# Smaller key tiles, larger table tiles and earlier splits at the start of a TensorE-bound attention

## The chip, the core and the metric

The kernel runs on one core of one Trainium2 chip. The metric is the device time in microseconds of one execution, as the median of several runs. A profile of one execution gives every instruction of the five engines (PE is TensorE, DVE is VectorE, ACT is ScalarE, POOL is GpSimd, SP is SyncE, which here only issues transfers) and every DMA. PEld is the loading of TensorE's weights, which overlaps its matmuls. The names ACT and DVE are used below as the profile uses them.

## What is computed

Eight images of 32 x 32 tokens with 384 channels pass through two layers. The start of the first layer is what matters here:

```
x = x + conv_attn(group_norm(x))
    qkv  = x @ qkv_w + qkv_b                 # 6 heads of 64
    attn = (q / 8) @ k.T                     # 1024 x 1024 per head
    attn += rel_h[query, key row] + rel_w[query, key column]
            # rel_h = q . rel_pos_h[hq - hk + 31], rel_w likewise
    x    = softmax(attn) @ v @ proj_w + proj_b
t = t + causal_attention(layer_norm(t))      # one head of 384
t = t + ffn(layer_norm(t))                   # sign weights; only images 0 to 4
```

## The kernel before, in words

An image b goes through layer 0 (projections, position tables, attention with 6 heads in 3 pairs), layer 1's attention, and for b = 0 to 4 through the FFN. Everything is fp32 or a pair of rounded values: q and k are each cut into a high part and the remainder, so that scores are the sum of three products: k with q, ks (k with its two parts exchanged) with q, and a fixed matrix `unit` with r, the position terms.

**PSUM.** Two pools: `ps_s` has 2 tiles of two banks (s tiles, 128 x 1024 in fp32), `ps_o` has 4 tiles of one bank (o tiles, 128 x 512).

**Projections of q and k** (`queries_keys`, L443). For m = 0 to 2 (q, one pair of heads each) and 3 to 5 (k), `project_T` (L383, matmuls L388) fills an s tile with 6 matmul instructions (12 records in the profile, since a matmul in full fp32 appears as two). Then for each half of 512 tokens ACT writes the high part with the bias (L453, two instructions of 64x512, one a head), and DVE writes the remainder from the same bank (L456, two instructions), which reads ACT's result. For k the parts are then copied by SP's transfers to `ks`.

**Position tables** (`positions`, L470). For a pair and a head (par) two o tiles of 512 queries are computed (L479) from q and a fixed table. ACT copies the upper 64 rows (L483) and DVE the lower 64 in column order (L484) into a page, which a transfer puts into DRAM (L488, `far`). Four transfers then read the diagonals back into one page `near` (L495), whose rows of 128 bytes put each query's 32 + 32 relevant values in place.

**Splits** (`split`, L500). `near` of a pair is cut into a high part, ACT's cast (L506), and a remainder, DVE's subtract (L507), both of 32x1024, four of each a pair, written into r. Those with d = 1 exchange rows and columns while they read. Pairs 0 and 1 are split next to the values; pair 2 is `later`, which the attention calls after its first group of products with v, except in image 0.

**Values** (`values`, L511). Eight blocks of 128 tokens in o tiles (L398), copied by ACT and DVE in turn (L512).

**Attention** (`attend0_fast`, L545). For each of 8 chunks of keys and each head of the pair: scores in an s tile (L554), exp on ACT into a page (L558), sums on DVE (L567), and two chunks behind, the products with v (L572).

**Order.** The source order gives each instruction its priority, and a scheduler fixes one stream for each engine. On its engine an instruction waits for those ahead of it. So an ACT instruction whose input is late holds up every ACT instruction behind it. The first q projections of image b + 1 are put into the stream of TensorE while image b's FFN ends. Its closing step (`finish`, L919 on DVE after L915 on POOL, then the output transfer L948) runs in the middle of the next image's projections, as `unfinished`. A function of another table set costs ACT an ACT_TABLE_LOAD: GELU (L854) and exp (L558) do, one after the other, in images 0 to 4 and the image that follows.

`multiply_out` (L282) computes wq @ wk.T once, in image 0, for layer 1: two loads and 9 matmul instructions; before, it comes at the end of image 0's projections.

Of the kernel before, what the change touches and what calls it, by code (L numbers as in the profile page):

```python
# [17 lines left out]
P = 128  # L18
# [56 lines left out]
def conv_attn_hybrid(  # L75
# [203 lines left out]
        nc.vector.tensor_tensor(pb, pb, ps[:, :C], ALU.add)  # L279


    def multiply_out(pools):  # L282
        both = pools.flat("wqkT")
        wqT_sb, wkT_sb = (both[:, i * NC * C : (i + 1) * NC * C].rearrange("p (k c) -> p k c", k=NC) for i in range(2))
        nc.sync.dma_start(out=wqT_sb, in_=wqT.rearrange("(k p) c -> p k c", p=P))
        nc.sync.dma_start(out=wkT_sb, in_=wkT.rearrange("(k p) c -> p k c", p=P))
        for m in range(NC):
            ps = pools.o_tile(f"wqk_{m}")
            for k in range(NC):
                nc.tensor.matmul(ps[:, :C], wqT_sb[:, k, ts(m, P)], wkT_sb[:, k, :], start=(k == 0), stop=(k == NC - 1))  # L290
            nc.vector.tensor_scalar_mul(wqk[:, m, :], ps[:, :C], C**-0.5)

    def stages(pools):
# [140 lines left out]
        def layer0(b, xT):  # L434

            q, k, ks, r = ([pools.image(f"{n}_{b}_{par}", F32R) for par in range(2)] for n in ("q", "k", "ks", "r"))

            rows = (slice(0, HD), slice(HD, P))

            def queries_keys(m):  # L443
                p = m % NPAIR
                bias = bqk[:, m : m + 1]
                ps = project_T(wqkv_sb, ts(m, P), xT, f"qk_{b}_{m}")
                dst = [(q if m < NPAIR else k)[par][:, p, :] for par in range(2)]

                for half in range(2):
                    t = ts(half, T // 2)  # L450
                    for par in range(2):
                        hi = rows[par]
                        nc.scalar.activation(dst[par][hi, t], ps[hi, t], AF.Identity, bias=bias[hi])  # L453
                    for par in range(2):
                        hi, lo = rows[par], rows[1 - par]
                        nc.vector.scalar_tensor_tensor(  # L456
                            dst[par][lo, t], ps[hi, t], bias[hi], dst[par][hi, t].bitcast(F32), ALU.add, ALU.subtract
                        )
                if m >= NPAIR:
                    for par in range(2):  # L460
                        for i in range(2):
                            nc.sync.dma_start(
                                out=ks[par][rows[i], p, :].bitcast(F32), in_=dst[par][rows[1 - i]].bitcast(F32)
                            )

            def positions(p):  # L470

                fars = []
                for par in range(2):
                    page = pools.page(f"far_{b}_{p}_{par}")
                    by_col = page.rearrange("i (w h) -> i w h", h=H)
                    for half in range(2):
                        ps = pools.o_tile(f"rel_{b}_{p}_{par}_{half}")
                        for i in range(2):
                            nc.tensor.matmul(  # L479
                                ps, rel_split[:, i].rearrange("d a n -> d (a n)"), q[par][:, p, ts(half, 512)],  # L480
                                start=(i == 0), stop=(i == 1),
                            )
                        nc.scalar.copy(page[:HD, ts(half, 512)], ps[:HD])  # L483
                        nc.vector.tensor_copy(  # L484
                            by_col[HD:, :, ts(half, H // 2)], ps[HD:].rearrange("i (h w) -> i w h", w=W)
                        )
                    far = store.tile([P, T], F32, tag=f"far_{p}_{par}", bufs=2, name=f"{pools.path}_far_{b}_{p}_{par}")
                    nc.sync.dma_start(out=far, in_=page)  # L488
                    fars.append(far)
                near = pools.page(f"near_{b}_{p}")  # L490
                for par in range(2):
                    start = fars[par][0:1, 0:1]
                    for d in range(2):
                        src = bass.AP(start.tensor, start.offset + d * HD * T, [[T, 32], [T + 32, 32], [1, 32]])
                        nc.sync.dma_start(  # L495
                            out=near[ts(2 * par + d, 32)].rearrange("m (n o) -> m n o", n=32), in_=src
                        )
                return near

            def split(p, near):  # L500
                for d in range(2):
                    for par in range(2):
                        hi, lo = 2 * par + d, 2 * (1 - par) + d
                        dst = r[par][:, p, :].rearrange("k (h w) -> k h w", h=H)
                        src = near[ts(hi, 32)].rearrange("k (w h) -> k h w" if d else "k (h w) -> k h w", h=H)
                        nc.scalar.copy(dst[ts(hi, 32)], src)  # L506
                        nc.vector.tensor_tensor(dst[ts(lo, 32)], src, dst[ts(hi, 32)].bitcast(F32), ALU.subtract)  # L507

            v = pools.flat(f"v0_{b}")[:, : NJ * C].rearrange("p (j c) -> p j c", j=NJ)

            def values(j):  # L511
                (nc.vector.tensor_copy if j % 2 else nc.scalar.copy)(  # L512
                    v[:, j, :], project(wqkv_sb, slice(2 * C, 3 * C), xT, j, f"v0_{b}_{j}")
                )

            near = []
            for m in range(2 * NPAIR):
                queries_keys(m)
                if 0 < m <= NPAIR:
                    near.append(positions(m - 1))  # L520
                if m == NPAIR and unfinished:
                    unfinished.pop()()
            split(0, near[0])
            for j in range(NJ):
                values(j)
            split(1, near[1])

            later = [lambda: split(2, near[2])]
            if b == 0 or not pools.fast:
                later.pop()()  # L530
            if pools.fast and b == 0:
                join_biases(pools)
                multiply_out(pools)

            def residual():
                xt = load_x(pools, b)
                nc.gpsimd.tensor_tensor(xt, xt, pb.unsqueeze(1).to_broadcast([P, NJ, C]), ALU.add)
                return xt
# [4 lines left out]
            return (attend0_fast if pools.fast else attend0_general)(residual, b, sides, v, later)  # L543

        def attend0_fast(residual, b, sides, v, later):  # L545


            oT = pools.image(f"oT_{b}")
# [75 lines left out]
            for p in range(NPAIR):  # L624
                sums = [pools.page(f"sum0_{b}_{p}_{par}") for par in range(2)]
                avs = None
                pending = []
                for c in range(NJ):
                    prs = [scores(p, c, par) for par in range(2)]
                    if c == 0:  # L630
                        first = prs
                    if c == 1:
                        if p > 0:
                            few = set_aside(p - 1, *last)
                        if p == 0 and b > 0:
                            xt = residual()
                        avs = [pools.o_tile(f"av0_{b}_{p}_{half}") for half in range(2)]
                    if b == 0 and (p, c) >= (0, 1) and xt is None and next(signs, True):
                        xt = residual()
                    if len(pending) == 2:  # L640
                        values(p, pending, sums, avs)
                        if later:
                            later.pop()()
                        if c == 4 and p > 0:
                            divide(p - 1, few)
                        pending = []
                    pending.append((c, prs))
                values(p, pending, sums, avs)
                last = (sums, avs)
# [18 lines left out]

            return xt, more

        def attend0_general(residual, b, sides, v, later):
            state = {}
            xt = residual()

# [173 lines left out]
        def ffn(xt, b):  # L848
# [71 lines left out]

            return add

        unfinished = []

        def run(pools):
            gn = load_T(0)
            if pools.fast:
                load_weights(pools)
            gn = group_norm_T(0, gn)
            if pools.fast:  # L930
                make_unit()
# [70 lines left out]
```

## Time and profile before

Three runs took 2600.14, 2606.68 and 2608.02 us; the median is 2606.68. The profiled execution has a span of 2599.5 us and a mean granted TensorE clock of 0.996.

| from the profile | |
|---|---|
| matmuls of q and k (L388) | 576 records, 261.5 us |
| matmuls of layer 0's scores (L554) | 3 x 768 records, 746.9 us |
| products with v (L572) | 1536 records, 359.7 us |
| exp of layer 0 (L558, ACT) | 384 instructions, 393.0 us |
| splits: ACT (L506), DVE (L507) | 96 of each, 145.9 and 193.7 us |
| transfers of k to ks | 96 of 256 KB, 5.1 us to landing |
| near, read from far | 96 of 128 KB, 3.9 us to landing |
| first projection of images 0 to 7 starts at | 16.9, 305.3, 654.5, 1003.6, 1352.4, 1700.4, 2048.3, 2319.8 us |

How to read it: a group's line has the source line, the engine and the operation, the tile written and the tiles read, the shape, then the busy time in us, the mean of one instruction in ns, and the engine's idle time just before these instructions, with what ended it. In a list of waits a line says which instruction of which engine waited for which other; numbers are the total in us, how often, and the longest. Idle time matters only on the engine that sets the end. An image with an FFN before it takes about 348 us, one without 271 to 280 (from the starts in the table).

### The profile page before, as it was taken

The page shows a single profiled execution, that of the slowest core. Times are in us where ns is not written, and L with a number is a line of the kernel's source. Part 1 is how long each engine was busy: PE and PEld are TensorE (multiplying, and loading weights), DVE is VectorE, ACT ScalarE, POOL GpSimd, SP SyncE. Part 2 cuts the span into 40 slices and gives each one's busy share as a digit, 9 for nine tenths or more (in the row PEclk, how much of TensorE's full clock was granted, in tenths as well). Part 3 has the DMA queues.
Part 4 walks back from the last instruction along what each step waited for, and adds up shares of the span by engine and source line. Part 5 has one row for each costly group of instructions (what it writes and reads, how often), then busy time and mean ns, then how long its engine had stood idle before and what let it go on. Part 6 is the DMA issues. An engine that isn't in the chain of part 4 may idle for free. (4 is left out here: it accounts for less than half of the span.)

```text
span 2599.5 us, 25162 instructions
## 1 busy us (share of the span) xinstructions
PE 2521.0 (97%) x9538; PEld 1508.4 (58%) x9538; DVE 1619.4 (62%) x2407; ACT 1157.0 (45%) x1513; POOL 115.5 (4%) x106
## 2 busy tenths in 40 slices
PE   7999998999999999999999999999999999999998
PEld 4555685555765556755557555576555555555554
DVE  5895468763587644786545776347864486538652
ACT  4641377421666314764127643156641264127420
POOL 1000002000001000010000100000100010001000
PEclk9999999999999999999999999999999999999999
DMA  6431106011042101150110601003200240015000
GB/s 167 147 146 61 37 1 170 1 61 37 1 117 54 49 13 37 41 130 1 61 37 1 170 1 61 6 31 91 80 25 1 67 104 1 25 39 131 1 1 26
DMA packets 148993, 144.72 MB, mean 56 GB/s; under 512 B 107264, under 2 KB 129664, under 8 KB 147328
## 3 DMA queue, kind: packets, MB, share of 16 engines
q1 hardware_dynamic: 142928, 119.36, 16.4%
q0 software_dynamic: 2880, 23.59, 2.6%
q8 instruction: 77, 1.26, 0.2%
q10 hardware_dynamic: 3056, 0.08, 0.1%
q14 instruction: 52, 0.43, 0.1%
HBM read 75.38 MB, written 42.47 MB: 45 GB/s over the span
## 5 line engine op out<-in xcount | busy, mean ns | idle before, releaser
L558 ACT ACTIVATE f_pr<-f_s 128x1024 f32<-128x1024 f32 x384 | 393.0, 1027 | 403.2 <-PE f_s L554 370.3
L567 DVE TENSOR_TENSOR f_sum<-f_sum,f_pr 128x1024 f32<-128x1024 f32 x288 | 349.0, 1244 | 147.0 <-ACT f_pr L558 145.6
L572 PE MATMUL f_av<-f_pr,f_v 128*64 128x512 f32 x1536 | 359.7, 599 | 0.0
L554 PE MATMUL f_s<-f_q,f_k 128*128 128x512 f32 x768 | 258.5, 418 | 21.8 <-ACT f_pr L558 14.9
L388 PE MATMUL f_qk<-f_gnT,wqkv_sb 128*128 128x512 f32 x576 | 261.5, 598 | 8.2 <-DVE f_k L456 5.6
L554 PE MATMUL f_s<-f_q,f_ks 128*128 128x512 f32 x768 | 245.3, 401 | 0.0
L554 PE MATMUL f_s<-f_r,unit 128*128 128x512 f32 x768 | 243.1, 398 | 0.0
L572 PEld LDWEIGHTS f_av<-f_pr,f_v 128*64 128x64 f32 x1536 | 103.2, 136 | 202.8 <-issue 195.0
L507 DVE TENSOR_TENSOR f_r<-f_near,f_r 32x1024 fp32r<-32x1024 f32 x96 | 193.7, 2017 | 29.0 <-ACT f_r L506 26.3
L554 PEld LDWEIGHTS f_s<-f_q,f_k 128*128 128x128 f32 x768 | 125.8, 189 | 137.9 <-issue 50.3
L762 PE MATMUL f_s<-f_q,f_lnT 128*128 128x512 f32 (+3 forms) x576 | 201.4, 491 | 0.0
L776 PE MATMUL f_av<-f_v,f_pr 128*128 128x385 f32 x576 | 194.5, 486 | 0.0
L388 PEld LDWEIGHTS f_qk<-f_gnT,wqkv_sb 128*128 128x128 f32 x576 | 108.0, 191 | 124.3 <-issue 114.0
L554 PEld LDWEIGHTS f_s<-f_q,f_ks 128*128 128x128 f32 x768 | 145.6, 190 | 35.9
L554 PEld LDWEIGHTS f_s<-f_r,unit 128*128 128x128 f32 x768 | 145.8, 190 | 34.8
L776 PEld LDWEIGHTS f_av<-f_v,f_pr 128*128 128x128 f32 x576 | 108.6, 190 | 78.6 <-issue 11.5
L506 ACT CAST f_r<-f_near 32x1024 fp32r<-32x1024 f32 x96 | 145.9, 1520 | 2.3
L398 PE MATMUL f_v<-wqkv_sb,f_gnT 128*128 128x384 f32 x384 | 129.4, 490 | 10.5 <-ACT f_v L512 8.3
L762 PEld LDWEIGHTS f_s<-f_q,f_lnT 128*128 128x128 f32 x576 | 100.1, 190 | 67.7 <-issue 43.5
L877 DVE TENSOR_REDUCE am<-f_h 128x1 f32<-128x1024 f32 (+2 forms) x80 | 71.6, 946 | 96.6 <-ACT f_h L870 96.6
L770 ACT ACTIVATE f_pr<-f_s 128x1024 f32<-128x1024 f32 (+3 forms) x64 | 41.7, 651 | 202.0 <-DVE f_s L767 202.0
L870 ACT ACTIVATE f_h<-f_y,b_sb 128x256 f32<-128x256 f32 x240 | 100.8, 472 | 67.0 <-PE f_y L866 67.0
(163 smaller groups left out, 3360.6 us busy)
## 6 DMA issues: line engine op xcount, KB each, us to landing
f_far<-f_far SPq DMA_DIRECT2D x48, 512.0 KB, 2.9
f_ks<-f_k SPq DMA_DIRECT2D x96, 256.0 KB, 5.1
f_gnT<-in_xT SPq DMA_DIRECT2D x24, 512.0 KB, 4.5
f_near<-f_far SPq DMA_DIRECT2D x96, 128.0 KB, 3.9
f_x<-in_x SPq DMA_DIRECT2D x32, 384.0 KB, 6.4
out_y<-f_x SPq DMA_DIRECT2D x32, 384.0 KB, 3.8
f_w1a<-w1s POOLq DMA_DIRECT2D x5, 1536.0 KB, 7.2
f_w2a<-w2s POOLq DMA_DIRECT2D x5, 1536.0 KB, 6.6
```

The lines of the kernel that those rows point to most:

```text
L388: nc.tensor.matmul(ps[:, half, :], w[:, k, cols], xT[:, k, ts(half, 512)], start=(k == 0), stop=(k == NC - 1),)
L398: nc.tensor.matmul(ps[:, :C], xT[:, k, ts(j, P)], w[:, k, cols], start=(k == 0), stop=(k == NC - 1))
L506: nc.scalar.copy(dst[ts(hi, 32)], src)
L507: nc.vector.tensor_tensor(dst[ts(lo, 32)], src, dst[ts(hi, 32)].bitcast(F32), ALU.subtract)
L554: nc.tensor.matmul(sc[:, half, :], keys[:, ts(c, P)], queries[:, ts(half, 512)], start=(i == 0), stop=(i == 2))
L558: nc.scalar.activation(pr, sc.rearrange("p a n -> p (a n)"), AF.Exp)
L567: nc.vector.tensor_tensor(sums[par], prev, prs[par], ALU.add)
L572: nc.tensor.matmul(avs[half][ts(par, HD), :], v[:, c, ts(h, HD)], prs[par][:, ts(half, 512)], start=(c == 0), stop=(c == NJ - 1),)
L762: nc.tensor.matmul(sc[:, half, lo:], xT[:, c // 4, k, ts(c % 4, P)], q[:, half, k, lo:], start=(k == 0), stop=(k == NC - 1),)
L776: nc.tensor.matmul(av[:, : C + 1], prs[c][:, ts(j - c, P)], v[:, c, :], start=(c == 0), stop=(c == j))
L870: nc.scalar.activation(pairs[i][:, m, :, :], ps[:, ts(i % 2, 256)].rearrange("p (j q) -> p j q", j=2), AF.Identity, bias=b1_sb[:, m : m + 1],)
L877: nc.vector.tensor_reduce(am[:, i, n - 1 : n], pairs[i][:, cuts[n - 1] : cuts[n], :, :], AX.XYZ, ALU.max, apply_absolute_value=True)
```

## The change

It rearranges what lies between an image's first projection and its first exponentials, so that TensorE finds its tiles and operands ready.

1. k, and in image 0 also q, is projected by halves into one-bank o tiles, so that ACT can take one half while DVE is at another. q of the other images stays in s tiles.
2. The table products of pairs 1 and 2 (in image 0 of all pairs) go to two-bank s tiles, and one ACT copy of 64x1024 and one DVE copy take the place of two each.
3. The splits of pairs 1 and 2 work on 64 rows at a time for both heads (`split_both`): two ACT copies and two DVE subtracts a pair into the pages of far, which are free by then, and eight transfers of 32x1024 from there into r. `near` is laid out by d for this. All splits stand ahead of the attention; `later` is gone. Pair 0 keeps `split`, called after the fifth projection.
4. After the previous image's closing step a one-element exp brings exp's table in (images 1 to 5).
5. wq and wk are loaded at the very start, and `multiply_out` runs after image 0's fifth projection.

```diff
-    def multiply_out(pools):
+    def load_qk(pools):
...
+        return wqT_sb, wkT_sb
+
+    def multiply_out(pools, wqT_sb, wkT_sb):
...
             def queries_keys(m):
                 p = m % NPAIR
                 bias = bqk[:, m : m + 1]
-                ps = project_T(wqkv_sb, ts(m, P), xT, f"qk_{b}_{m}")
                 dst = [(q if m < NPAIR else k)[par][:, p, :] for par in range(2)]
 
+                both = project_T(wqkv_sb, ts(m, P), xT, f"qk_{b}_{m}") if b and m < NPAIR else None
                 for half in range(2):
                     t = ts(half, T // 2)
+                    if both is None:
+                        ps = pools.o_tile(f"qk_{b}_{m}_{half}")
+                        for i in range(NC):
+                            nc.tensor.matmul(
+                                ps, wqkv_sb[:, i, ts(m, P)], xT[:, i, t], start=(i == 0), stop=(i == NC - 1)
+                            )
+                    else:
+                        ps = both[:, t]
...
             def positions(p):
 
-                fars = []
+                fars, pages = [], []
                 for par in range(2):
                     page = pools.page(f"far_{b}_{p}_{par}")
+                    pages.append(page)
                     by_col = page.rearrange("i (w h) -> i w h", h=H)
-                    for half in range(2):
-                        ps = pools.o_tile(f"rel_{b}_{p}_{par}_{half}")
...
+
+                    n = 1 + (p > 0 or b == 0)
+                    for part in range(2 // n):
+                        ps = pools.s_tile(f"rel_{b}_{p}_{par}") if n == 2 else pools.o_tile(f"rel_{b}_{p}_{par}_{part}")[:, None, :]
...
+                        ps = ps.rearrange("p a n -> p (a n)")
+                        nc.scalar.copy(page[:HD, ts(part, n * 512)], ps[:HD])
                         nc.vector.tensor_copy(
-                            by_col[HD:, :, ts(half, H // 2)], ps[HD:].rearrange("i (h w) -> i w h", w=W)
+                            by_col[HD:, :, ts(part, n * H // 2)], ps[HD:].rearrange("i (h w) -> i w h", w=W)
                         )
...
+                        at = 2 * d + par if p else 2 * par + d
+                        nc.sync.dma_start(out=near[ts(at, 32)].rearrange("m (n o) -> m n o", n=32), in_=src)
+                return near, [page.bitcast(F32R) for page in pages]
+
+            def split_both(p, near, pages):
+
+                for d in range(2):
+                    hi, lo, src = (t[ts(d, HD)].rearrange("k (h w) -> k h w", h=H) for t in (*pages, near))
+                    if d:
+                        src = near[ts(d, HD)].rearrange("k (w h) -> k h w", h=H)
+                    nc.scalar.copy(hi, src)
+                    nc.vector.tensor_tensor(lo, src, hi.bitcast(F32), ALU.subtract)
+                for i in range(2):
+                    for d in range(2):
+                        for par in range(2):
+                            nc.sync.dma_start(
+                                out=r[par][ts(2 * i + d, 32), p, :].bitcast(F32),
+                                in_=pages[i][ts(2 * d + par, 32)].bitcast(F32),
+                            )
...
                 queries_keys(m)
                 if 0 < m <= NPAIR:
                     near.append(positions(m - 1))
+                if m == NPAIR + 1 and sides_qk:
+                    multiply_out(pools, *sides_qk.pop())
                 if m == NPAIR and unfinished:
                     unfinished.pop()()
-            split(0, near[0])
+
+                    early = pools.small.tile([P, 1], F32, tag="early", name=f"early0_{b}")
+                    nc.scalar.activation(early, k[1][:, 0, T - 1 :].bitcast(F32), AF.Exp, scale=0.0)
+                if m == NPAIR + 1:
+                    split(0, near[0][0])
             for j in range(NJ):
                 values(j)
-            split(1, near[1])
-
-            later = [lambda: split(2, near[2])]
-            if b == 0 or not pools.fast:
-                later.pop()()
+            split_both(1, *near[1])
+            split_both(2, *near[2])
             if pools.fast and b == 0:
                 join_biases(pools)
-                multiply_out(pools)
...
                     if len(pending) == 2:
                         values(p, pending, sums, avs)
-                        if later:
-                            later.pop()()
...
             if pools.fast:
                 load_weights(pools)
+                sides_qk.append(load_qk(pools))
```

More of the change, by code (lines that the diff above doesn't have):

```diff
@@ L445, in queries_keys @@
                 bias = bqk[:, m : m + 1]
-                ps = project_T(wqkv_sb, ts(m, P), xT, f"qk_{b}_{m}")
                 dst = [(q if m < NPAIR else k)[par][:, p, :] for par in range(2)]
+                both = project_T(wqkv_sb, ts(m, P), xT, f"qk_{b}_{m}") if b and m < NPAIR else None
                 for half in range(2):
                     t = ts(half, T // 2)
+                    if both is None:
[6 more added lines that the diff above has]
+                        ps = both[:, t]
                     for par in range(2):
                         hi = rows[par]
-                        nc.scalar.activation(dst[par][hi, t], ps[hi, t], AF.Identity, bias=bias[hi])
+                        nc.scalar.activation(dst[par][hi, t], ps[hi], AF.Identity, bias=bias[hi])
                     for par in range(2):
@@ L456, in queries_keys @@
                         nc.vector.scalar_tensor_tensor(
-                            dst[par][lo, t], ps[hi, t], bias[hi], dst[par][hi, t].bitcast(F32), ALU.add, ALU.subtract
+                            dst[par][lo, t], ps[hi], bias[hi], dst[par][hi, t].bitcast(F32), ALU.add, ALU.subtract
                         )
@@ L470, in positions @@
             def positions(p):
-                fars = []
+                fars, pages = [], []
                 for par in range(2):
                     page = pools.page(f"far_{b}_{p}_{par}")
+                    pages.append(page)
                     by_col = page.rearrange("i (w h) -> i w h", h=H)
-                    for half in range(2):
-                        ps = pools.o_tile(f"rel_{b}_{p}_{par}_{half}")
[L478 to L483, printed above, removed]
+                    n = 1 + (p > 0 or b == 0)
+                    for part in range(2 // n):
+                        ps = pools.s_tile(f"rel_{b}_{p}_{par}") if n == 2 else pools.o_tile(f"rel_{b}_{p}_{par}_{part}")[:, None, :]
+                        for half in range(n):
+                            for i in range(2):
+                                nc.tensor.matmul(
+                                    ps[:, half, :], rel_split[:, i].rearrange("d a n -> d (a n)"),
+                                    q[par][:, p, ts(part + half, 512)], start=(i == 0), stop=(i == 1),
+                                )
+                        ps = ps.rearrange("p a n -> p (a n)")
+                        nc.scalar.copy(page[:HD, ts(part, n * 512)], ps[:HD])
                         nc.vector.tensor_copy(
-                            by_col[HD:, :, ts(half, H // 2)], ps[HD:].rearrange("i (h w) -> i w h", w=W)
+                            by_col[HD:, :, ts(part, n * H // 2)], ps[HD:].rearrange("i (h w) -> i w h", w=W)
                         )
@@ L494, in positions @@
                         src = bass.AP(start.tensor, start.offset + d * HD * T, [[T, 32], [T + 32, 32], [1, 32]])
[L495 to L498, printed above, removed]
+                        at = 2 * d + par if p else 2 * par + d
[8 more added lines that the diff above has]
+                    nc.vector.tensor_tensor(lo, src, hi.bitcast(F32), ALU.subtract)
+                for i in range(2):
+                    for d in range(2):
[3 more added lines that the diff above has]
+                                in_=pages[i][ts(2 * d + par, 32)].bitcast(F32),
+                            )
             def split(p, near):
@@ L542, in layer0, with attend0_fast @@
                       for par in range(2)] for p in range(NPAIR)]
-            return (attend0_fast if pools.fast else attend0_general)(residual, b, sides, v, later)
-        def attend0_fast(residual, b, sides, v, later):
+            return (attend0_fast if pools.fast else attend0_general)(residual, b, sides, v)
+        def attend0_fast(residual, b, sides, v):
             oT = pools.image(f"oT_{b}")
@@ L669, in attend0_fast, with attend0_general @@
             return xt, more
-        def attend0_general(residual, b, sides, v, later):
+        def attend0_general(residual, b, sides, v):
             state = {}
@@ L921, in ffn @@
             return add
+        sides_qk = []
         unfinished = []
```

## The prediction

> **What bounds the kernel.** First the page's part 1, then the waits of PE (total us, times, longest), then the groups, then the timeline of one image's start.
>
> ```profile
> PE 2521.0 (97%) x9538; PEld 1508.4 (58%) x9538; DVE 1619.4 (62%) x2407; ACT 1157.0 (45%) x1513; POOL 115.5 (4%) x106
> ```
>
> ```profile
> PE f_s L554 <- ACT f_pr L558: 14.9, 13, 1.9
> ...
> PE f_v L398 <- ACT f_v L512: 8.3, 8, 1.1
> PE f_qk L388 <- DVE f_k L456: 5.6, 5, 2.3
> ...
> PE f_s L554 <- DVE f_k L456: 4.1, 5, 0.8
> ...
> PE f_s L554 <- ACT f_far L483: 2.8, 3, 0.9
> PE f_v L398 <- DVE f_far L484: 2.2, 5, 0.4
> ...
> PE f_qk L388 <- DVE f_q L456: 1.5, 5, 0.3
> ```
>
> TensorE does its 2521 us whatever happens; only its idle 78.5 us can be won. The seven waits shown, all between an image's projections and its first exponentials, sum to 39.4 us. The groups say why (busy, mean ns, then idle before):
>
> ```profile
> L453 ACT ACTIVATE f_k<-f_qk,bqk 64x512 fp32r<-64x512 f32 x96 | 65.5, 683 | 86.9 <-DVE f_k L456 56.0 <-PE f_qk L388 29.8
> L456 DVE SCALAR_TENSOR_TENSOR f_k<-f_qk,bqk,f_k 64x512 fp32r<-64x512 f32 x96 | 71.9, 749 | 40.7 <-ACT f_k L453 38.9
> ```
>
> ACT's second half of a k tile waits for DVE's first half: the two engines take turns on a two-bank tile. A tile costs 4 x 0.68 + 4 x 0.75 = 5.7 us in turn, while TensorE fills it in 12 records of 0.43 us start to start, 5.15 us. One image's start (image 3, timeline of PE; start, duration, idle before in brackets):
>
> ```profile
> 1108.53 5.39 PE L388 MATMUL f_qk<-f_gnT,wqkv_sb 128*128 128x512 f32 x12 [0.61 <-DVE f_k L456]
> 1114.75 0.71 PE L554 MATMUL f_s<-f_q,f_k 128*128 128x512 f32 x2 [0.82 <-DVE f_k L456]
> 1115.89 8.01 PE L398 MATMUL f_v<-wqkv_sb,f_gnT 128*128 128x384 f32 x24 [0.44 <-DVE f_far L484]
> ...
> 1127.34 6.07 PE L398 MATMUL f_v<-wqkv_sb,f_gnT 128*128 128x384 f32 x18 [1.05 <-ACT f_v L512]
> ...
> 1137.14 0.73 PE L554 MATMUL f_s<-f_q,f_k 128*128 128x512 f32 x2 [1.87 <-ACT f_pr L558]
> ```
>
> These idle 4.79 us; a modelled end hides about 0.15 more of each gap, so 5.5 us. Right after the last one the clock drops (windows; the columns are length, busy PE, PEld, DVE, ACT, POOL, clock, DMA share, GB/s):
>
> ```profile
> 1138.00:1142.00 4.00, 4.00 (x11) 2.64 (x10) 1.22 (x1) 3.65 (x4) 0.00 (x0) 0.57 1.00 341
> ```
>
> 4 x (1 - 0.57) = 1.7 us more. Image 3 loses 7.2 us here. By the same reading image 0 loses 6.4 (idle of 0.92, 1.02, 0.92, 1.45 and 1.29, and 5 x 0.15), images 1 to 5 lose 7.7, 8.4, 7.2, 7 and 7, images 6 and 7, which come after no FFN, 3.4 each (0.92, 1.03, 0.43, 0.35, and 4 x 0.15): about 50 us, the ceiling of the change. Images 2 to 5 show the half clock; 1, 6 and 7 don't. The 1.87 us wait is ACT's table load:
>
> ```profile
> 1120.66 6.13 ACT L506 CAST f_r<-f_near 32x1024 fp32r<-32x1024 f32 x4
> ...
> 1134.77 1.28 ACT L558 ACT_TABLE_LOAD   x1
> 1136.06 1.94 ACT L558 ACTIVATE f_pr<-f_s 128x1024 f32<-128x1024 f32 x2
> ```
>
> **The Trainium skill.** "PSUM — Partial Sum Buffer", Terms: two engines collide when they touch the same bank and quadrant of 32 partitions. The two halves of a k tile are different banks, so the 56.0 us of turn-taking is wider than the page requires: it is the tile that is guarded, and one-bank tiles remove it. "ScalarE activation tables: per-element evaluation and per-set limits", What a function is on this engine: functions of different sets are a 1283 ns load apart; the trace has 1.28. "TensorE: Matmul & The Clock Gate", Part 1: after an idle window of about 3.4 us the clock is half; the window runs freely. The trace agrees with half speed, and that it strikes after some stalls of 2 us and not others fits a free window.
>
> **The change, part by part.**
>
> 1. k (and image 0's q) by halves in one-bank tiles. Same matmuls (5.15 us a block). ACT needs 2.7 and DVE 3.0 us a block and can now overlap on different tiles, both under 5.15, so the waits on f_k and f_q go: 5.6 + 4.1 + 1.5 = 11.2 us.
>
> 2. Table products of pairs 1, 2 in two-bank tiles. Not in the trace; "VectorE: DVE Perf Modes", the TRN2 errata table, gives (172 + 1024)/1.2 = 1.0 us for ACT and (120 + 1024)/0.96 = 1.2 for DVE (its 512 forms, 0.57 and 0.66, are measured at 0.58 and 0.69). Upper bound: two old ones, 1.16 and 1.39. I take 1.0 and 1.2, estimates; hidden under k's matmuls. It frees o tiles (2.8 + 2.2 us of waits on far go), but adds a wait: the second product of pair 1 needs the s tile of q's third block, whose turn-taking lasts 5.7 us after its last matmul. Between lie one product (4 x 0.23 = 0.9), one k half (2.6) and part of another (1.3): 4.8 us. New wait 0.9 us in images 1 to 5; with one far copy in between, 1.75 in images 6, 7.
>
> 3. Splits. Per image 12 ACT casts (1.52 mean) and 12 DVE subtracts (2.02) become 8 and 8, the new ones 64x1024 at the same length; ACT saves about 6, DVE 8 us an image. Both work under TensorE at 97%: nothing. 16 DMAs of 128 KB more an image (3.9 us each to land, as f_near): 2.1 MB, some 6 us at 341 GB/s, and first needed at pair 1, 40 us later: nothing. But the order: the instructions of the changed program put one split of pair 1 (1.0 us contiguous) on ACT's queue ahead of split(0)'s 6.1 us and v0's copy. Behind it wait v0's evacuation and, four o tiles on, v4's matmuls. From the end of k's last half TensorE has v0 to v3 (4 x 1.94) and two score halves (1.1), 8.9 us; ACT has the two table copies left over and the last k half (2.4 + 1.4), 1.0, 6.1 and 0.4, 11.3. Wait 2.4 us instead of 1.05 in images 1 to 5; about 1.3 in 6, 7; 0.6 in image 0.
>
> 4. Early exp table, images 1 to 5: 1.28 us goes to a place where ACT waits for DVE anyway; the 1.87 becomes about 0.25. Behind it in ACT's queue is the fourth k block, with four o tiles (10.3 us of matmuls) of slack.
>
> 5. wq @ wk.T: 18 matmuls of 0.32 us, 5.8 us, moved; nothing. In image 0 they and the missing late split take away the 0.92, 1.45 and 1.29 us exp waits.
>
> Sum. Images 1 to 5: loss after 0.9 + 2.4 + 0.3 = 3.6. If the half clock goes too, the mean 7.5 becomes 3.6, 3.9; scores also start on a filled pipe (the later split no longer sits between exponentials), some 0.3: 4.2 x 5 = 21. Image 0: 6.4 to 1.4, 5. Images 6, 7: 1.75 + 1.3 + 0.25 = 3.3 for 3.4: 0. In all 26 of 50 us: 2606.7 - 26 = 2581 us.
>
> **Rivals.**
> - Nearly all goes (new waits under 0.5 us, because table copies are short and near lands early): 50 - 8 x 0.7 = 44: 2563. For it: ACT is 45% busy. Against: ACT is full in just these 30 us.
> - Half: the v4 wait of 2.4 us still trips the half clock in four or five images (back 1.7 x 5 = 8.5), or the new waits are 1.5 times mine (8 us back): gain 17 to 9, 2590 to 2597.
> - No change: new waits double (3.3 x 7 = 23 back), 2604.
> - Slower: near of pair 1 lands late. Its split stands at the head of ACT's queue, so lateness goes straight to v0 and v4. DMA's share between 1106 and 1141 us is 92%, where k's copies, near's short rows and the new transfers meet. 5 us late in 8 images is 40: +14, 2621. Against: near of pair 1 was issued at 1108 us and lands in 3.9, before ACT comes there.
>
> **Numbers.** Main case 0.5 (2572 to 2588), nearly all 0.13, half 0.2, no change 0.07, slower 0.1. So 2581; range 2562 to 2602; faster 0.83, same 0.07, slower 0.10.
>
> **What would show it.** Right: waits of PE on f_k gone; ACT's k evacuation waits for PE alone; no table load between scores and the first exp; PE busy within 2 us of 2521; f_v <- ACT at 12 to 16 us; a new 0.9 us wait of rel on q's evacuation. Wrong if that last or f_v's wait is over 20 us, if half-clock stretches remain after the stalls, or if the DMA-fed split waits for near.

## The result

The changed kernel takes 2586.75 us (median of 4 runs, 2585.38 to 2587.49) against 2607.35 us for the kernel before (2600.14 to 2608.29); the ratio is 0.9926, with a 95% interval of 0.9908 to 0.9945. The forecast was 2581, in a range of 2562 to 2602. The profiled executions have spans of 2599.5 and 2585.6 us, so the traces have 13.9 us to explain; before's profiled execution was one of its shorter ones.

The total lies near the forecast, but only in part for the reasons given. A table shows it, each image taken from its first table product to that of the next image (from the starts of these products in the timeline of PE; image 7 to the end of the span):

| image | before, us | after, us | gain | forecast |
|---|---|---|---|---|
| 0 | 362.11 | 377.71 | -15.6 | +5 |
| 1 | 349.11 | 344.56 | 4.5 | 4.2 |
| 2 | 349.48 | 344.17 | 5.3 | 4.2 |
| 3 | 348.49 | 344.66 | 3.8 | 4.2 |
| 4 | 348.02 | 344.86 | 3.2 | 4.2 |
| 5 | 271.62 | 267.41 | 4.2 | 4.2 |
| 6 | 271.44 | 267.74 | 3.7 | 0 |
| 7 | 269.80 | 264.64 | 5.2 | 0 |

Images 1 to 7 gain 29.9 us, image 0 loses 15.6, and 0.4 is lost ahead of the first product.

### The profile page after: what moved, and what is told of

Its sections match the earlier page's. It is cut to its first block, busy times and chain, and to the rows that moved or that the text cites. A ratio compares the mean times of both kernels' runs of the same rounds, so it can differ in the third digit from the quotient of the medians.

```text
span 2585.6 us, 25377 instructions
## 1 busy us (share of the span) xinstructions
PE 2519.0 (97%) x9538; PEld 1510.1 (58%) x9538; DVE 1559.6 (60%) x2341; ACT 1104.3 (43%) x1452; POOL 107.3 (4%) x106
## 4 chain that ended last, share of the span: by engine, by line
PE 87%; ACT 5%; DVE 4%; issue 1%; DMA 1%; POOL 0%; SPq 0%; ACTq 0%; POOLq 0%
PE f_s L587 20%; PE f_av L605 12%; PE f_v L401 8%; PE f_s L793 7%; PE f_av L807 7%; PE f_y L897 6%; PE f_qk L457 5%; PE f_q L755 5%; PE f_y L936 4%; PE f_qk L391 4%; PE f_pj L401 2%; PE f_rel L494 2%; PE f_pj L690 2%; ACT f_r L537 1%; PE f_pt L303 1%
## 5 line engine op out<-in xcount | busy, mean ns | idle before, releaser
L600 DVE TENSOR_TENSOR f_sum<-f_sum,f_pr 128x1024 f32<-128x1024 f32 x288 | 385.5, 1371 | 150.3 <-ACT f_pr L591 148.9
L807 PEld LDWEIGHTS f_av<-f_v,f_pr 128*128 128x128 f32 x576 | 108.8, 190 | 78.4 <-issue 11.5
L755 PE MATMUL f_q<-f_lnT,wqk 128*128 128x512 f32 x288 | 127.5, 593 | 0.0
L401 PE MATMUL f_v<-wv_sb,f_lnT 128*128 128x384 f32 x384 | 126.5, 486 | 0.0
```

The source lines that it names most:

```text
L401: nc.tensor.matmul(ps[:, :C], xT[:, k, ts(j, P)], w[:, k, cols], start=(k == 0), stop=(k == NC - 1))
L600: nc.vector.tensor_tensor(sums[par], prev, prs[par], ALU.add)
L755: nc.tensor.matmul(ps, wqk[:, k, ts(m, P)], xT[:, half, k, :], start=(k == 0), stop=(k == NC - 1))
L807: nc.tensor.matmul(av[:, : C + 1], prs[c][:, ts(j - c, P)], v[:, c, :], start=(c == 0), stop=(c == j))
```

## The profile after

Part 1 of the page, and from the waits of PE those that the text uses:

```profile
PE 2519.0 (97%) x9538; PEld 1510.1 (58%) x9538; DVE 1559.6 (60%) x2341; ACT 1104.3 (43%) x1452; POOL 107.3 (4%) x106
```

```profile
PE f_den L647 <- DVE f_sum L600: 11.5, 1, 11.5
PE f_gmean L326 <- DVE gmv L321: 10.1, 3, 6.3
PE f_s L587 <- ACT f_pr L591: 9.8, 17, 1.2
PE f_den L635 <- ACT f_oT L624: 5.7, 1, 5.7
...
PE f_v L401 <- ACT f_v L543: 0.9, 5, 0.2
```

Of the seven waits that the prediction summed to 39.4 us, those on k and on the tables are gone, f_v's wait is 0.9 us for 8.3, that on exp 9.8 for 14.9, and that on q of the early blocks stays (1.4). Two single waits are new, 11.5 and 5.7 us, both at the denominators of layer 0's attention, and both in image 0. Before, the list had one wait there:

```profile
PE f_den L614 <- DVE f_sum L567: 0.9, 1, 0.9
```

The groups of k's evacuation:

```profile
L464 ACT ACTIVATE f_k<-f_qk,bqk 64x512 fp32r<-64x512 f32 x96 | 65.5, 682 | 41.5 <-PE f_qk L457 40.3
L467 DVE SCALAR_TENSOR_TENSOR f_k<-f_qk,bqk,f_k 64x512 fp32r<-64x512 f32 x96 | 71.9, 749 | 21.1 <-ACT f_k L464 18.9
```

The instructions take what they took. What ended ACT's idle time was DVE for 56.0 us before; now it is TensorE alone. ACT and DVE no longer take turns on k.

Image 3 on TensorE and on ACT, for the stretch shown of before:

```profile
1110.45 8.75 PE L457 MATMUL f_qk<-f_gnT,wqkv_sb 128*128 128x512 f32 x20
1119.03 8.06 PE L401 MATMUL f_v<-wqkv_sb,f_gnT 128*128 128x384 f32 x24
...
1130.11 6.07 PE L401 MATMUL f_v<-wqkv_sb,f_gnT 128*128 128x384 f32 x18 [0.17 <-ACT f_v L543]
...
1138.22 0.73 PE L587 MATMUL f_s<-f_q,f_k 128*128 128x512 f32 x2 [0.18 <-ACT f_pr L591]
```

```profile
1110.40 1.28 ACT L558 ACT_TABLE_LOAD   x1 [1.76 <-DVE f_k L467]
...
1123.40 6.16 ACT L537 CAST f_r<-f_near 32x1024 fp32r<-32x1024 f32 x4
1129.58 0.86 ACT L543 COPY f_v<-f_v 128x384 f32<-128x384 f32 x2
```

Five waits of 4.79 us have become two of 0.35. The table load has moved ahead, behind a wait of 1.76 us for DVE. The clock is full in the window in which it was 0.57 (columns as in the prediction; here the first exponentials run in it too):

```profile
1138.00:1142.00 4.00, 3.82 (x17) 3.07 (x17) 0.00 (x0) 2.81 (x4) 0.00 (x0) 1.00 1.04 230
```

Not all of this reaches the end of the image. In image 3 the first score product of pair 1 with r starts 79.8 us after the first table product, for 85.6 before: 5.8 us ahead. The last such product of the attention starts after 151.9 us for 155.9, 4.0 ahead. TensorE's timeline at the start of pair 1 shows one cause:

```profile
1174.10 0.74 PE L587 MATMUL f_s<-f_q,f_k 128*128 128x512 f32 x2
1174.67 0.63 PE L587 MATMUL f_s<-f_q,f_ks 128*128 128x512 f32 x2
1175.14 0.62 PE L587 MATMUL f_s<-f_q,f_k 128*128 128x512 f32 x2
1175.60 0.64 PE L587 MATMUL f_s<-f_q,f_ks 128*128 128x512 f32 x2
1176.07 0.62 PE L587 MATMUL f_s<-f_r,unit 128*128 128x512 f32 x2
1177.80 0.50 PE L587 MATMUL f_s<-f_q,f_k 128*128 128x512 f32 x1 [1.11 <-ACT f_pr L591]
```

In images 1 to 5 the written order there computes k and ks of two score tiles and only then r of the first, so the first exp starts late, both tiles are full, and TensorE waits. In images 6 and 7, and in every other chunk but the first of an image, the order is k, ks, r of one tile. That r comes last fits its new way, by transfers; that the scheduler therefore reckoned it late is argued, not shown.

**Image 0.** SyncE's queue, before and after (start, duration of the issues with their waits, source line, transfer):

```profile
75.22 27.21 SPq L233 DMA_DIRECT2D f_w<-in_w1T  x2
102.48 1.26 SPq L233 DMA_DIRECT2D f_w<-in_w2T  x2
```

```profile
69.25 26.64 SPq L526 DMA_DIRECT2D f_r<-f_far  x16
95.98 1.08 SPq L233 DMA_DIRECT2D f_w<-in_w1T  x2
97.12 41.74 SPq L233 DMA_DIRECT2D f_w<-in_w2T  x2
```

The FFN weights, which image 0 turns into signs while its attention runs, are loaded behind the 16 transfers into r. DVE's timeline, before and after:

```profile
98.69 1.48 DVE L240 TENSOR_REDUCE sums_w<-f_w 128x1 f32<-128x614 f32 x2
...
189.10 13.47 DVE L567 TENSOR_TENSOR f_sum<-f_sum,f_pr 128x1024 f32<-128x1024 f32 x6
```

```profile
134.86 7.36 DVE L240 TENSOR_REDUCE sums_w<-f_w 128x1 f32<-128x614 f32 x15
...
203.92 13.35 DVE L600 TENSOR_TENSOR f_sum<-f_sum,f_pr 128x1024 f32<-128x1024 f32 x6
```

The first reduction runs 36 us later, though its data were issued only some 20 us later. DVE had 23 us of work between 80 and 120 us and 33 before, and is then busy nearly to the end of the attention; its last six sums start 15 us later. TensorE waits for them. Between 200 and 220 us it is busy for 8.50 us, for 18.52 before (columns as in the prediction):

```profile
200.00:220.00 20.00, 18.52 (x62) 9.28 (x59) 16.62 (x37) 0.68 (x2) 0.86 (x1) 1.00 0.29 105
200.00:220.00 20.00, 8.50 (x29) 2.89 (x27) 17.94 (x11) 3.08 (x3) 7.92 (x2) 0.75 0.63 226
```

DVE, 60% busy over the span, is the bound of image 0's last third. The clock adds to the loss: within each of the two long waits it falls to half, at 148.5 us for 6.8 us and at 209.9 us for 10.2 us, where image 0 of before has no half clock. TensorE is busy for 7.3 us of these 17.1, so they cost about 3.6 us more (an estimate from these times).

## The experiments

All times are medians of 4 runs; ratios are to the kernel before, run beside them. Spans are those of the profile. The tables were not all measured beside the same runs of the kernel before, so between tables ratios and spans say more than medians. Each table has its runs in the order of the edits above it. Where only a few instructions move, the images' lengths in the trace tell more than the total.

**Image 0, three ways.** The theory is that the work on the FFN weights comes late. The rival is that image 0's new tiles and products are slow in themselves.

```diff
-                            nc.sync.dma_start(
+                            (nc.sync if b else nc.gpsimd).dma_start(
                                 out=r[par][ts(2 * i + d, 32), p, :].bitcast(F32),
```

> The changed kernel, but in image 0 the 16 transfers of pairs 1 and 2 into r are issued by GpSimd instead of SyncE, so the FFN weight loads behind them on SyncE's queue are issued some 25 us earlier and the order written for VectorE has the weight reductions in pair 0 again (after chunk 5) instead of pair 1. Image 0, from its first table product to image 1's: 362.1 us before, 377.7 after. Theory 'late weight work' (the reductions and signs of the FFN weights start 30 us late on VectorE, so its sums of the last pair run late and TensorE waits 5.7 and 11.5 us at the two denominators): image 0 takes 357 to 362, the total falls by 16 to 20 to 2567 to 2571, and both waits at the denominators fall below 1.5 us. Rival 'image 0 is slow by its new tiles' (q and all tables of image 0 in other PSUM tiles, wq @ wk.T among the projections): image 0 stays at 376 to 378 and the total at 2586.

```diff
-            split_both(1, *near[1])
-            split_both(2, *near[2])
+            for p in (1, 2):
+                split_both(p, *near[p]) if b else split(p, near[p][0])
...
-                        at = 2 * d + par if p else 2 * par + d
+                        at = 2 * d + par if p and b else 2 * par + d
```

> The changed kernel, but image 0 splits pairs 1 and 2 with the old 32-row split straight into r (8 casts and 8 subtracts, no transfers into r). Theory 'late weight work': image 0 back to 358 to 364 us; a little worse than with GpSimd's queue, since ACT and VectorE do 4 more instructions each of 1.5 to 2 us between the first exponentials, so waits of scores on exp of up to 3 us come back; total 2568 to 2574. Rival 'new tiles': image 0 at 376 to 378, total 2586.

```diff
-                if m == NPAIR + 1 and sides_qk:
-                    multiply_out(pools, *sides_qk.pop())
...
                 join_biases(pools)
+                multiply_out(pools, *load_qk(pools))
...
-                sides_qk.append(load_qk(pools))
```

> The changed kernel, but the two loads and the products of wq @ wk.T stand at their old place after image 0's projections. SyncE still issues the 16 transfers into r ahead of the FFN weight loads, but the order written for VectorE has the weight reductions behind pair 0's chunk 4, not in pair 1. Two forms of the theory differ here. 'Written order': what costs is that VectorE's fixed order puts the reductions 30 us later than the data is there (the loads are issued at 96 to 97 us, the reductions run at 135): image 0 returns to 358 to 364, total 2568 to 2574. 'Late data': what costs is the loads' place on SyncE's queue, so VectorE now waits in front of the reductions with the sums queued behind: image 0 stays over 372, total over 2582. 'New tiles' says no change, 2586, as well.

| run | median, us | ratio (95%) | image 0, us | images 1 to 5, us |
|---|---|---|---|---|
| img0_pool | 2574.14 | 0.9895 (0.9873 to 0.9917) | 364.6 | 344.5 to 344.8, 267.4 |
| img0_split | 2576.87 | 0.9904 (0.9882 to 0.9926) | 367.3 | 344.4 to 344.8, 267.4 |
| img0_wqk_late | 2573.27 | 0.9884 (0.9861 to 0.9908) | 363.6 | 344.5 to 345.0, 267.6 |

All three bring image 0 back by 10 to 14 us and leave the other images alone, so its new tiles aren't the cause. The first misses the 357 to 362 that was expected of it, and the second its 358 to 364. The waits at the denominators fall to 3.3 and 4.0 us with GpSimd's queue, not under 1.5; in the third run one of 0.5 us is left. The third run separates order from data (its timelines of SyncE and of DVE):

```profile
70.38 18.18 SPq L526 DMA_DIRECT2D f_r<-f_far  x16
...
89.87 14.49 SPq L233 DMA_DIRECT2D f_w<-in_w1T  x2
```

```profile
102.55 2.18 DVE L240 TENSOR_REDUCE sums_w<-f_w 128x1 f32<-128x614 f32 x3
```

The transfers into r still stand ahead of the loads, which go out 6 us earlier than in the changed kernel. But the reductions run 32 us earlier, since DVE's written order has them behind chunk 4 of pair 0 instead of in pair 1, and DVE waits for data only 0.29 us there. So what cost 14 us is the written order, as far as these runs go. The loads' place on the queue counts in so far as it shifts that order. Why the place of wq @ wk.T shifts it too isn't settled.

**The early table, taken out.**

```diff
-                    early = pools.small.tile([P, 1], F32, tag="early", name=f"early0_{b}")
-                    nc.scalar.activation(early, k[1][:, 0, T - 1 :].bitcast(F32), AF.Exp, scale=0.0)
```

> The changed kernel without the early one-element exp in images 1 to 5: the table of exp is loaded where the first real exponential stands. Theory (the load was worth its 1.28 us and the half clock that follows): the second score tile's wait on exp goes from 0.2 to 1.3 to 1.9 us in images 1 to 5, and where the clock falls another 1.7: 7 to 18 us in all, total 2593 to 2604. Rival 'hidden anyway' (ACT now has 2 us of idle time ahead of the first exp, so the load fits in there): less than 2 us, total 2586 to 2588.

2583.29 us, ratio 0.9929 (0.9907 to 0.9952): the same as with it. Images 1 to 5 are 0.6 to 0.8 us shorter without (image 3: 343.9 for 344.7), and no half clock returns between image 1 and the last 10 us of the span. The wait of the second score tile is 0.2 us with and without; in image 3 without:

```profile
1136.33 0.73 PE L584 MATMUL f_s<-f_q,f_k 128*128 128x512 f32 x2 [0.20 <-ACT f_pr L588]
```

In this kernel the load was hidden anyway, as the rival said: ACT waits another 1.07 us for TensorE after it. So here the early table is not what took the 1.87 us and the half clock away. What it costs shows at the start of pair 1, where image 3's wait is 1.11 us with it and 0.42 without.

**One part of the change undone in images 1 to 7.**

```diff
-                both = project_T(wqkv_sb, ts(m, P), xT, f"qk_{b}_{m}") if b and m < NPAIR else None
+                both = project_T(wqkv_sb, ts(m, P), xT, f"qk_{b}_{m}") if b or m < 0 else None
```

> The changed kernel with k (and image 0's q) projected into two-bank tiles again, all else as changed. Images 1 to 7, from first table product to first table product, took 349.1, 349.5, 348.5, 348.0, 271.6, 271.4, 269.8 before and 344.6, 344.2, 344.7, 344.9, 267.4, 267.7, 264.6 after, 4.3 less on average. Theory 'k tiles carry it': TensorE's waits on f_k come back (2 to 3 us an image: ACT and VectorE take turns on a tile, and the two-bank tables now want the same tiles), images 1 to 7 take 2 to 4 us more each, total 2600 to 2612. Rival 'the splits carry it' (what mattered is that fewer split instructions stand ahead of the first exponentials): under 1 us an image, total 2586 to 2592.

(Image 0's q and k stay in one-bank tiles in this run, against what the expectation says.)

```diff
-                    n = 1 + (p > 0 or b == 0)
+                    n = 1 + (b == 0)
```

> The changed kernel with the table products of pairs 1 and 2 in one-bank tiles (two copies each), as before, in images 1 to 7. Theory: they now compete with k's halves for the four one-bank tiles, and each copy is shorter but there are more of them: 0.5 to 2 us an image, total 2588 to 2600. Rival 'hidden': ACT and VectorE have slack there, under 0.3 us an image, total 2585 to 2588.

```diff
-            split_both(1, *near[1])
-            split_both(2, *near[2])
+            for p in (1, 2):
+                split(p, near[p][0]) if b else split_both(p, *near[p])
...
-                        at = 2 * d + par if p else 2 * par + d
+                        at = 2 * d + par if p and not b else 2 * par + d
```

> The changed kernel with the old 32-row splits straight into r in images 1 to 7 (12 casts and 12 subtracts an image for 8 and 8, no transfers into r), pair 2 still ahead of the attention in the source. Theory 'the splits carry part': pair 1's four casts (6 us on ACT) stand near the values and the first exponentials again, so TensorE waits for exp 1 to 2 us an image, with the half clock behind it in some images (1.7 each): 1 to 4 us an image, total 2594 to 2615. Rival 'hidden': with k's waits gone ACT has the time, under 0.5 us an image, total 2585 to 2590.

| run | median, us | ratio (95%) | images 1 to 4, us | images 5, 6, 7, us |
|---|---|---|---|---|
| k_two_bank | 2687.88 | 1.0319 (1.0287 to 1.0352) | 358.9 to 361.2 | 283.7, 279.1, 276.0 |
| rel_one_bank | 2644.23 | 1.0153 (1.0120 to 1.0185) | 351.4 to 354.0 | 274.3, 275.2, 272.2 |
| split_small | 2577.08 | 0.9894 (0.9863 to 0.9926) | 341.9 to 342.3 | 264.8, 269.0, 266.1 |

The first two are slower than the kernel before, and lose several times what was expected (101 and 57 us in the median against the changed kernel). The waits of PE say what happens when both k and the tables use one pool, two-bank first, one-bank second:

```profile
PE f_s L587 <- DVE f_r L538: 22.4, 7, 3.2
PE f_rel L494 <- DVE f_k L467: 18.8, 7, 3.4
...
PE f_qk L391 <- DVE f_far L500: 9.8, 5, 2.6
```

```profile
PE f_qk L457 <- DVE f_far L500: 26.4, 12, 2.7
...
PE f_v L401 <- ACT f_v L543: 10.2, 14, 1.2
PE f_rel L494 <- DVE f_k L467: 7.9, 8, 1.6
```

Tables wait for k's evacuation and k for the tables'. The first line, scores that wait for the split of pair 0, is not explained by this alone. A good part of the loss is the clock: for the same matmuls TensorE is busy for 2560.7 and 2536.9 us, 41.7 and 17.9 more than in the changed kernel, at a mean granted clock of 0.980 and 0.989 for 0.995. So the two edits aren't two gains but one exchange: k leaves the two-bank pool, the tables take its place. The third run went the other way, by 10.5 us of span: the old splits are *better* by 2.3 to 2.6 us in images 1 to 5 and worse by 1.3 to 1.5 in images 6 and 7. With them the wait at pair 1's start is gone, and the order there is k, ks, r again; so it is the new splits that bring the late r about. The wait is 1.1 us of the 2.3 to 2.6; the rest isn't traced.

**The exchange alone, and undone as a pair.** The first is the kernel before with the diffs of parts 1 and 2 of the change and nothing else; the second is the changed kernel with the two one-line edits of k_two_bank and rel_one_bank together.

> The kernel before with the two tile edits alone: k (and image 0's q) in one-bank tiles, the tables of pairs 1 and 2 (of all pairs in image 0) in two-bank tiles. Splits, exp's table and wq @ wk.T as before. Theory 'the exchange of tiles carries the gain' (each of the two edits undone alone cost 7 to 15 us an image, since both then crowd one pool, so they work as a pair): images 1 to 5 at 343 to 345, images 6 and 7 at 266 to 268, image 0 at 359 to 362, total 2566 to 2574. Rival 'the splits and their order carry half': images 1 to 5 at 346 to 348, total 2585 to 2595.

> The changed kernel with both tile edits undone together in images 1 to 7 (k in two-bank, tables in one-bank tiles); splits, exp's table and wq @ wk.T as changed. Theory 'the exchange of tiles carries the gain': images 1 to 7 return to 347 to 350 and 270 to 272, total 2603 to 2618, far less than the sum of the two undone alone (+101 and +57). Rival 'the splits carry half': 345 to 347 an image, total 2592 to 2603.

| run | median, us | ratio (95%) | image 0, us | images 1 to 4, us | images 5, 6, 7, us |
|---|---|---|---|---|---|
| tiles_only | 2563.04 | 0.9856 (0.9829 to 0.9883) | 359.1 | 343.0 to 343.2 | 266.1, 268.9, 265.3 |
| tiles_back | 2627.55 | 1.0106 (1.0077 to 1.0135) | 376.9 | 349.4 to 352.2 | 274.8, 272.7, 267.6 |

The exchange of tiles alone gives more than the whole change: 38.6 us of span for 13.9, and the intervals of the ratios lie apart. Both totals missed what was expected (2566 to 2574 and 2603 to 2618): the exchange gave more, and undoing it cost more. The trace of tiles_only has no half clock before the last 10 us, although exp's table is loaded at the first exponential as in the kernel before. The remaining parts without it (image 0's tiles stay as changed) are worse than the kernel before, by 14.8 us in image 0 and by 0.3 to 3.7 in images 1 to 6; image 7 is 2.2 shorter. They do not carry half the gain; they cost.

With the changed splits and order in, four runs show what each move does alone. Their spans are 2625.1 us with neither (tiles_back), 2640.4 with k moved (rel_one_bank), 2679.4 with the tables moved (k_two_bank) and 2585.6 with both (the changed kernel). So k's move alone costs 15.3 us, that of the tables alone 54.3, and both together win 39.5. The cost of k's move alone is the weakest of these: the ratios' intervals of rel_one_bank and tiles_back overlap. Neither move was run alone on the kernel before.

**What was of use.**

> The changed kernel with wq @ wk.T at its old place and without the early exp: what the two earlier runs found harmful, both undone. If the effects add: image 0 at 363 to 364, images 1 to 5 at 343.5 to 344.2, total 2568 to 2572, about 1.2 per cent under the kernel before. If the order written for image 1 onward shifts with it: anything up to 2576.

The diffs of img0_wqk_late and no_early together: 2569.22 us, ratio 0.9863 (0.9832 to 0.9895); image 0 takes 363.3 us and images 1 to 4 343.7 to 344.4. The two effects add.

> The changed kernel with the old 32-row splits in images 1 to 7, wq @ wk.T at its old place and no early exp: all that the earlier runs found of no use, undone, and the tiles and the order of the splits kept. If the effects add (image 0 from 377.7 to 363.5; images 1 to 5 from 344.6 to about 341.7, images 6 and 7 at 266 to 269): total 2553 to 2562. If the order written for each engine shifts once more: up to 2570, which would show that the parts don't add.

The same with split_small's diff: 2565.80 us, ratio 0.9863 (0.9836 to 0.9891), span 2564.2. Images 1 to 5 are at 342.6 to 343.0 and 265.7, not 341.7: against split_small they are 0.3 to 1.1 us longer, though taking out the early table had made them shorter in the changed kernel. These parts don't add, and the total missed the 2553 to 2562 expected.

```diff
                 if m == NPAIR and unfinished:
                     unfinished.pop()()
+
+                    early = pools.small.tile([P, 1], F32, tag="early", name=f"early0_{b}")
+                    nc.scalar.activation(early, k[1][:, 0, T - 1 :].bitcast(F32), AF.Exp, scale=0.0)
```

> The kernel before with the two tile edits and the early exp, nothing else. Against the two tile edits alone (images 1 to 5 at 343.0 us, profile 2560.9) it tells what the early table is worth where no other edit stands beside it. Theory 'of no use' (taken out of the changed kernel, images 1 to 5 became 0.6 to 0.8 us shorter): 343.0 to 343.8, total 2561 to 2567. Rival 'useful where the first exponentials are not held up by splits': up to 1.3 us less in images 1 to 5, 341.7 to 342.9, total 2554 to 2560.

This is tiles_only with the early table: 2557.34 us (2556.04 to 2559.26), ratio 0.9830 (0.9812 to 0.9848), the fastest of all, and its interval lies clear of the changed kernel's. It overlaps that of tiles_only; that the early table is of use here rests on the traces. Images 1 to 5 are 1.0 to 1.2 us shorter than in tiles_only, and the wait of the second score tile shows why (image 3, tiles_only and this run):

```profile
1117.21 0.74 PE L565 MATMUL f_s<-f_q,f_k 128*128 128x512 f32 x2 [1.27 <-ACT f_pr L569]
```

```profile
1113.01 0.73 PE L568 MATMUL f_s<-f_q,f_k 128*128 128x512 f32 x2 [0.18 <-ACT f_pr L572]
```

With the old splits ACT is busy right up to the load, so the load is not hidden.

The waits of PE that are left in it, over 2 us:

```profile
PE f_gmean L323 <- DVE gmv L318: 9.9, 3, 6.1
PE f_s L568 <- ACT f_pr L572: 6.6, 17, 1.4
PE f_pt L300 <- DVE xn L377: 5.5, 16, 0.4
PE f_y L919 <- DVE f_lo L906: 4.1, 5, 0.8
PE f_y L919 <- ACT f_hi L904: 4.0, 15, 0.4
```

All but the second lie outside the stretch that the change is about. The wait on exp is 12.1 us in tiles_only and 6.6 here.

## Why the prediction was right, and where it was not

The forecast of 26 us was 20.6 in the medians and 13.9 in the traces. By its steps:

1. **k in one-bank tiles: right.** ACT and DVE work side by side, the waits on k are gone, and the profile shows the sign that was named; only q's wait of 1.5, part of the step's 11.2 us, stays at 1.4. But the step counted the edit as worth 11.2 us by itself. rel_one_bank, which keeps it and leaves the tables where they were, is 1.5% slower than the kernel before, with the other parts of the change in it, and 15.3 us of span longer than tiles_back, which has neither. The prediction never asked what k's halves do to the one-bank pool if the tables stay there.
2. **Tables in two-bank tiles: the durations were right, the new wait did not come.** An ACT copy took 1.00 us and a DVE copy 1.23, for estimates of 1.0 and 1.2 from "VectorE: DVE Perf Modes" of the Trainium skill, the TRN2 errata table. The second product of pair 1 was to wait 0.9 us for q's tile. In image 3 it starts at 1104.68 us, without a wait, before DVE has finished with q (1105.95), and 0.4 us after DVE's copy of the product before it (1103.01 and 1.23). So it does not use q's tile but, by these times, the one that the product before it left. The step assumed that two tiles are handed out in turn.
3. **Splits at nothing: wrong on both sides.** The v wait was to be 2.4 us an image and is 0.17 in image 3. ACT was as busy as reckoned (11.0 us from the first v product to the end of v0's copy, for 11.3), but TensorE had one more block of values to do before it needed that tile: 10.75 us of its own, for 8.9. Against that, the transfers were not free. The step counted their bytes and their landing and never what stands behind them on SyncE's queue and what the scheduler makes of it: 10 to 14 us in image 0, by the three runs. In images 1 to 5 the new splits cost 2.3 to 2.6 us each, by split_small. The written order of DVE for image 0 could have been read beforehand; the prediction read TensorE's and ACT's.
4. **The early table: the wait fell to 0.2 as forecast, but would have without it.** no_early has the same 0.2, since the new splits leave ACT idle time at that place. With the exchange of tiles and the old splits (tiles_only) the wait is 1.3 us, and the half clock is gone all the same; there the early table takes the wait to 0.2 and is worth about 1 us an image (tiles_early). Beside the new splits it costs 0.6 to 0.8.
5. **wq @ wk.T at nothing: wrong by the same 14 us.** Moving it back, with the transfers kept, restores image 0 to 363.6, so the loss needs both, and undoing either is enough. What the step said of image 0's waits on exp (0.92, 1.45 and 1.29 us) came true: its start keeps one of 0.2.

**Sum.** Images 1 to 5 gained 21.1 us for a forecast of 21, but this is a balance, and so luck: two waits that did not come (2.4 and 0.9) against a loss in pair 1 that was not foreseen. Images 6 and 7 gained 8.9 for a forecast of 0, since both waits expected there stayed away. Image 0 was forecast at +5 and came at -15.6. That these two errors have opposite signs is luck too.

The sign "PE busy within 2 us of 2521" came true (2519.0), but the busy time is not the fixed amount that the prediction took it for: it is 2509.8 us in tiles_only and 2560.7 in k_two_bank, for the same matmuls. It holds half clocks, in which a pair of score products takes 1.05 us for 0.63 (image 3 of before, 1138 to 1141 us). The sign "half-clock stretches remain" was to show the prediction wrong, and in image 0 they came new.

Of the rivals, "nearly all goes" (2563) was right on the new waits, which stay under 0.5 us at an image's start. In gain, images 1 to 7 lie midway with 29.9 us, between the forecast's 21 and about 39 by that rival (44.1 less 7 x 0.7). tiles_only comes nearest to its 44: it takes 35.9 us less than the kernel before beside it. The slower rival named near's late landing; near still lands in 3.8 us, and nothing waited for it on the path.

## What to carry to other kernels

When a pool of accumulator tiles is short, look at which groups share it before pricing any one move. Moving one group between pools can be worse than moving none, while exchanging two can remove the waits of both. Where a scheduler writes the engines' orders, an edit that is free in time can still move distant work, so read the new order of every engine, not only of the ones that the edit touches, and above all what stands behind an added transfer. And take a bundle of edits apart: here one pair of five parts gave more than all of them together.

## What was not expected of the hardware

- In images 2 to 5 of the kernel before, TensorE's clock was at half for 3.41 us, each time right after the wait on exp. The windows of image 3 just ahead of that stretch and in it, then one of image 1 (columns as in the prediction):

```profile
1134.68:1138.09 3.41, 1.54 (x7) 0.98 (x6) 2.65 (x3) 3.36 (x5) 0.00 (x0) 1.00 1.03 220
1138.09:1141.50 3.41, 3.41 (x10) 2.36 (x8) 1.22 (x1) 3.08 (x3) 0.00 (x0) 0.50 1.06 366
438.36:441.77 3.41, 1.57 (x7) 1.30 (x8) 2.05 (x2) 3.38 (x4) 0.00 (x0) 1.00 1.03 276
```

In all four images the 3.41 us ahead of the half clock hold the whole wait (1.85 to 1.87 us), and TensorE is busy for 1.54 to 1.56 of them. "TensorE: Matmul & The Clock Gate" of the Trainium skill, Part 1, speaks of an idle window of about 3.4 us. The length agrees: the four stretches start at 789.93, 1138.09, 1486.25 and 1834.41 us, each 102 times 3.413 us after the one before. But the window need not be idle throughout; here one that was idle for a little over half was enough. Where the limit lies isn't shown: counted on the same grid, image 1 has a window with 1.57 us busy and keeps its full clock. In tiles_only the wait is 1.3 us, and no half clock follows from image 1 to the last 10 us.
- Six sums on DVE took 13.35 to 13.47 us at the end of image 0, before and after. Five of them took 1.2 us each, as elsewhere; one took 7.80 us (7.67 after). It started while GpSimd's addition of 128x3072 was running (7.21 and 7.11 us), and ended 1.1 us after it. The same is seen in all eight images of both kernels: the one DVE instruction that starts during this addition takes 6.0 to 7.8 us and ends 1.1 to 1.8 us after it, in images 1 to 7 a subtract of the splits before and a sum after, which take 1.2 to 2.0 us elsewhere. That it waits for the addition is read from these times; no run moved the addition. The change didn't alter this; in image 0 it moved DVE's work up to it.
